# q of a deformable-attention layer by seven products of halves instead of eight, placed in the middle of an even round

## The chip, the cores and the metric

The kernel runs on one core of one Trainium2 chip. The metric is the time of one execution on the device, in microseconds (us). Several runs of the same kernel give a median; one further execution was taken with a profile, and all durations of single instructions come from that one. Engines are named as in the profile: PE is TensorE's matmul, PEld its weight load, DVE is VectorE, ACT is ScalarE, POOL is GpSimd, SP is SyncE, which here only issues DMAs.

## What is computed

Two layers act on x, of 8 images with 512 channels of 64 x 64 pixels, all float32. Cut to what matters here:

```
x = x + attention(group_norm(x))
x = x + bottleneck(group_norm(x))

attention(x):
    q  = w_q @ x                      # 512 x 512 times 512 x 4096 pixels, per image
    t  = gelu(q[every 4th pixel] * w_off1 + b_off1)
    positions = grid + 4 * tanh(w_off2 @ t)        # per group of 64 channels
    f  = bilinear samples of q at the positions    # 256 per group
    k, v = split(w_kv @ f)
    out  = softmax(0.125 * q^T k) v                # 8 heads of 64, 256 keys
    return w_out @ out + b_out
```

The change touches only how q = w_q @ x is formed, and when.

## The kernel before

Everything is float32 and lies in SBUF as 128 partitions x 4 channel blocks x pixels. An image is cut into 8 tiles `t` of 512 pixels (`TP`). An image's tiles lie in nine places of 512 pixels; x of tile t lies in place t + 1 and q of tile t in place t, so q of one tile overwrites x of the tile before it.

**One image's attention is 32 rounds** (8 tiles x 4 pairs of heads, `names`, index `g`, with `r = g % 32`). Round g issues, in this order on PE: the weighted values `pa` (L475), on even rounds the softmax denominators `pn` (L502) of the two rounds before, the logits `ps` of round g + 1 (L457) whose exponentials ACT writes into `es`, and the output projection `pp` (L544) of round g - 6 (`LAG`). DVE adds two exponentials per round (L487), scales, adds the residual (L551) and takes statistics (L554). After each of two places in a round `fill` advances a generator, `next_image`, which carries the work that lies beside: the second layer of the image before (`layer1`), loading and normalising the next image, its q, and its sampling (`sample`).

**q of an image** is `project_q`. Per tile it issues 16 matmuls of 128 x 128 weights on 512 columns (four output blocks of four accumulating matmuls, L252), ACT copies each output block from PSUM (L259), POOL normalises the next tile (L208, four instructions; tile 0 is DVE's), and behind each output block `by_pixel` transposes a quarter of the tile before on PE (four transposes, L226), copies it on ACT or DVE in turn (L236, L234) and stores it to DRAM (L237, on SP's queue) where `sample` gathers from it. At the end of a tile DVE takes the largest magnitude of q (L265). The yields of `project_q` sum to less than the 200 that one call of `fill` may spend, so a whole image's q stands on PE as one unbroken block. For images 2 to 7 this block lies in round 19, between the logits and the output projection. The q of image 0 and of image 1 lie ahead of the first round; that of image 1 is mixed with the sampling of image 0 (L927 to L930).

**Sampling** (`sample`) takes slots that alternate between the two places of a round: gathers issued by POOL (L396), weighing on DVE (L362 to L367), and twice `to_channels`, which transposes on PE (L372) and copies on ACT (L377). In round 30 what is left is drained and `project_k` follows (L410, 16 matmuls of 128 x 128 weights on 256 columns), which reads the copies.

The four buffers `es` (128 x 1024 each) hold exponentials. After the sum of round g's two exponentials on an even round, three of them are free. `wbuf` holds w_q while q is made, and w_kv otherwise. PSUM has two tiles of two banks (`ps_s`), two of one bank (`ps_mm`), and one bank each for `pa` and `pn`.

Of the kernel before, what the change touches and what calls it, by code (L numbers as in the profile page):

```python
# [8 lines left out]
F32 = mybir.dt.float32  # L9
# [7 lines left out]
P = 128  # L17
# [32 lines left out]
def kernel(  # L50
# [50 lines left out]
    def x_tile(b, t):  # L101
        return spot(b, t + 1)

    def q_tile(b, t):
        return spot(b, t)
# [33 lines left out]
        nc.sync.dma_start(wbuf, wv[:, :, part * C : (part + 1) * C])  # L139

    def load_weights_late():
        nc.sync.dma_start(wout, w_outT.rearrange("(cc p) o -> p cc o", p=P))
        nc.sync.dma_start(convw, conv_wT.rearrange("(cc p) o -> p cc o", p=P))
        nc.sync.dma_start(outw, out_wT)
        nc.sync.dma_start(fc2b, fc2_bias)

    def col(k, n=1):
        return vec[:, k : k + n]
# [47 lines left out]
                nc.vector.bn_stats(st[:, cc, t, :], x_tile(b, t)[:, cc, :])  # L196
                yield None

    def project_q(b, st, mq, qd, pools):

        gs = yield from group_stats(st, 0, b)

        qd_px = qd.rearrange("(g h p j) d -> h p g (j d)", g=HEADS, p=P, j=2)

        def normalise(t):
            xt = x_tile(b, t)
            for cc in range(NCC):
                (nc.gpsimd if t else nc.vector).tensor_scalar(  # L208
                    xt[:, cc, :],
                    xt[:, cc, :],  # L210
                    gs[:, 0, cc : cc + 1],
                    gs[:, 1, cc : cc + 1],
                    ALU.subtract,
                    ALU.mult,
                )

        def by_pixel(t, k, bank=(ps_a, "pa")):

            h, ch = divmod(k, 2)
            px = q_tile(b, t)[:, :, 2 * P * h : 2 * P * (h + 1)].rearrange(  # L220
                "p c (n j) -> p c j n", j=2
            )
            pt = bank[0].tile([P, 2, 2 * P], F32, tag=bank[1], name=f"pqt_{b}_{t}_{k}")
            for j in range(2):
                for i in range(2):
                    nc.tensor.transpose(  # L226
                        pt[:, j, i * P : (i + 1) * P], px[:, 2 * ch + i, j, :], ident
                    )
            pool, tag = pools[k % len(pools)]
            qr = pool.tile([P, C], F32, tag=tag, name=f"qr_{b}_{t}_{k}")  # L230
            qr_out = qr.rearrange("p (g j d) -> p j g d", j=2, d=DH)
            qr_in = pt.rearrange("p j (g d) -> p j g d", d=DH)
            if k % 2:
                nc.vector.tensor_copy(qr_out, qr_in)  # L234
            else:
                nc.scalar.copy(qr_out, qr_in)  # L236
            nc.sync.dma_start(  # L237
                qd_px[2 * t + h, :, 4 * ch : 4 * ch + 4, :],
                qr.rearrange("p (g m) -> p g m", g=4),
            )  # L240

        yield None
        normalise(0)
        yield None
        for t in range(NT):
            xt, qt = x_tile(b, t), q_tile(b, t)
            if t + 1 < NT:
                normalise(t + 1)
            for oc in range(NCC):
                pq = ps_mm.tile([P, TP], F32, tag="mm", name=f"pq_{b}_{t}_{oc}")  # L250
                for cc in range(NCC):
                    nc.tensor.matmul(  # L252
                        pq,
                        wbuf[:, cc, oc * P : (oc + 1) * P],
                        xt[:, cc, :],
                        start=(cc == 0),
                        stop=(cc == NCC - 1),
                    )
                nc.scalar.copy(qt[:, oc, :], pq)  # L259
                yield 4  # L260
                if t:
                    by_pixel(t - 1, oc)
                    yield 0.64
            if mq is not None:
                nc.vector.tensor_reduce(  # L265
                    mq[:, t, :], qt, axis=AX.X, op=ALU.max, apply_absolute_value=True
                )
        for q in range(NQ):
            by_pixel(NT - 1, q, ((ps_a, "pa"), (ps_mm, "mm"))[q % 2])
            yield 0.64  # L270
# [8 lines left out]
    def sample(b, qd):  # L279
# [101 lines left out]

        steps = [(h, half, ky) for h in range(2) for half in range(2) for ky in range(2)]

        for slot in range(2 * len(steps) + 4):
            n, odd = divmod(slot, 2)
            if odd and n >= 5 and n % 4 == 1:
                to_channels(n // 4 - 1)
            if odd and 1 <= n <= len(steps):
                weigh(*steps[n - 1], held.pop(0))
            if n < len(steps):  # L390
                h, half, ky = steps[n]
                if not odd:
                    held.append(gp.tile([P, 4, 2, DH], F32, tag="g", name=f"g_{b}_{n}"))
                for i in (2 * odd, 2 * odd + 1):
                    k = h * HEADS + 4 * half + i
                    nc.gpsimd.indirect_dma_start(  # L396
                        held[-1][:, i, :, :].rearrange("p j d -> p (j d)"),
                        None,
                        qd[:, :],
                        bass.IndirectOffsetOnAxis(ap=row[:, ky, k : k + 1], axis=0),  # L400
                    )
            yield None
# [457 lines left out]
    def next_image(b):  # L860

        n = b + 1
        if b:
            free = spot(b - 1, 0)
            first = layer1(b - 1, st1s.pop(b - 1), project_beside, free, free[:, 0:2, :])
            other, blocks = iter(()), ()
            if n < B:
                st = new_stats(0, n)
                blocks = norm_x(n, st)
                other = ready_q(n, st)  # L870


            first_load = 5
            ahead = 4
            slot = 0
            while first:
                if blocks is None and ahead:
                    next(other)
                    ahead -= 1
                if next(first, "end") == "end":  # L880
                    first = None
                if n < B:
                    if first_load <= slot < first_load + NT:
                        load_x(n, (slot - first_load,), nc.gpsimd)
                    if slot == first_load + 2 * NT:
                        load_wq()
                    if phase[0] and (slot == first_load + 3 or slot > first_load + 6):
                        for _ in range(4 if slot == first_load + 3 else 5):
                            if blocks and next(blocks, "end") == "end":
                                blocks = None  # L890
                slot += 1
                yield None
            yield from other
        if n < B:
            yield from sample(n, qds[n])

    qds = {}

    def ready_q(n, st):
        qds[n] = dpool.tile([N * HEADS, DH], F32, tag="qd", name=f"qd_{n}")  # L900
        mqs[n] = small.tile([P, NT, NCC], F32, tag=f"mq{n % 2}", name=f"mq_{n}")
        yield from project_q(n, st, mqs[n], qds[n], both_pools if n > 1 else both_pools[:1])
        if n:
            load_wkv(0)

    with tc.manual_schedule():
        load_x(0)
# [9 lines left out]
        st = new_stats(0, 0)  # L917
        drain(norm_x(0, st))

        for n, step in enumerate(ready_q(0, st)):  # L920
            if n == 3 * NCC:
                st = new_stats(0, 1)
                blocks, other = norm_x(1, st), ready_q(1, st)
            if n >= 3 * NCC and next(blocks, "end") == "end" and 13 * NCC <= n < 13 * NCC + 4:
                next(other)
        room = 0
        for step in sample(0, qds[0]):  # L927
            room += 7
            while room > 0:
                room -= next(other, 7) or 7  # L930
        project_k(0, mqs.pop(0), wkv[0])
        drain(other)
        logits(*names[0])
        project_v(0, wkv[1])
        for g in range(len(names) + LAG):
# [18 lines left out]
                sum_exps(*names[g - 1])  # L954
            if g < len(names):
                add_exps(*names[g])
            if summed:
                invert(*names[g - 1])
            if g + 1 < len(names):
                logits(*names[g + 1])  # L960
# [43 lines left out]
    with tc.If(large > 0):  # L1004
        with tc.For_i(0, B, 1) as i:
            b = "m"
            place[b], region[b] = i, 0
            qd = dpool.tile([N * HEADS, DH], F32, tag="qd", name=f"qd_{b}")
            load_wq()
            load_x(b)  # L1010
            st0, st1 = new_stats(0, b), new_stats(1, b)
            drain(norm_x(b, st0), project_q(b, st0, None, qd, both_pools), sample(b, qd))
            load_wkv(0)
            project_k(b, None)
            project_v(b)
            for t in range(NT):
                attention_max(b, t)
                for oc in range(NCC):
                    load_residual(b, t, oc)
                    project_out(b, t, oc, st1)  # L1020
            drain(layer1_last(b, st1, 1))
# [79 lines left out]
```

## Time and profile before

| what | us |
|---|---|
| median of 3 runs | 3431.71 (3426.51 to 3434.96) |
| the profiled execution, its own time | 3412.4 |
| its span, first to last instruction | 3410.6 |
| PE busy | 3321.9 (97%), 16660 matmuls |
| DVE busy | 1895.9 (56%) |
| ACT busy | 1088.9 (32%) |
| POOL busy | 965.1 (28%) |
| PE busy on the q products, L252 | 920.4, of 2048 records |
| PE busy on the output projection, L544 | 822.9 and 118.6 (two places of the operand) |
| mean granted TensorE clock | 0.99 |

A float32 matmul shows as two records of the same shape, one after the other. "Busy" is the time in which an engine has an instruction running; records of matmuls overlap, so the time that one adds is read from the distance between starts. In the lists, a line gives start, length, engine, source line, operation, output and inputs with partitions x elements, and in brackets how long the engine had been idle before it and what ended that.

### The profile page before, as it was taken

The page shows a single profiled execution, that of the slowest core. Times are in us where ns is not written, and L with a number is a line of the kernel's source. Part 1 is how long each engine was busy: PE and PEld are TensorE (multiplying, and loading weights), DVE is VectorE, ACT ScalarE, POOL GpSimd, SP SyncE. Part 2 cuts the span into 40 slices and gives each one's busy share as a digit, 9 for nine tenths or more (in the row PEclk, how much of TensorE's full clock was granted, in tenths as well). Part 3 has the DMA queues.
Part 4 walks back from the last instruction along what each step waited for, and adds up shares of the span by engine and source line. Part 5 has one row for each costly group of instructions (what it writes and reads, how often), then busy time and mean ns, then how long its engine had stood idle before and what let it go on. Part 6 is the DMA issues. An engine that isn't in the chain of part 4 may idle for free.

```text
span 3410.6 us, 42081 instructions
## 1 busy us (share of the span) xinstructions
PE 3321.9 (97%) x16660; PEld 1242.5 (36%) x16660; DVE 1895.9 (56%) x2958; ACT 1088.9 (32%) x1505; POOL 965.1 (28%) x726
## 2 busy tenths in 40 slices
PE   6999999999999999999999999999999999999996
PEld 3554323335332353324433244322443325433222
DVE  5433765752757427583375923668246682566665
ACT  1223332342333323233233423334233342333420
POOL 6181400162301713027040270302712036210201
PEclk9999999999999999999999999999999999999996
DMA  7222222662326523274333833247232572322713
GB/s 278 74 77 65 81 75 63 197 138 68 118 87 209 110 78 112 75 223 105 93 88 105 217 90 108 88 139 187 70 109 79 183 159 61 107 84 77 125 42 133
DMA packets 293183, 390.35 MB, mean 114 GB/s; under 512 B 17649, under 2 KB 157169, under 8 KB 292977
## 3 DMA queue, kind: packets, MB, share of 16 engines
q1 hardware_dynamic: 240368, 261.72, 23.9%
q0 software_dynamic: 52608, 125.86, 16.6%
q8 instruction: 132, 2.16, 0.3%
q14 instruction: 75, 0.61, 0.1%
HBM read 193.52 MB, written 192.94 MB: 113 GB/s over the span
## 4 chain that ended last, share of the span: by engine, by line
PE 88%; issue 4%; DVE 3%; DMA 2%; ACT 1%; POOL 1%; SPq 0%; ACTq 0%; POOLq 0%; DVEq 0%
PE pq L252 26%; PE pp L544 24%; PE ps L457 12%; PE pa L475 12%; PE pn L502 3%; PE pqt L226 3%; PE py L627 2%; PE pk L410 2%; PE pv L437 2%; PE po L770 2%; DMA out_dram<-spare 1%; DMA out_dram<-image 1%; DMA rn<-rn 1%; DVE wbuf L674 0%; PE po L304 0%
## 5 line engine op out<-in xcount | busy, mean ns | idle before, releaser
L252 PE MATMUL pq<-image,wbuf 128*128 128x512 f32 x2048 | 920.4, 595 | 2.5 <-DVE image L208 1.9
L544 PE MATMUL pp<-image,wout 128*64 128x512 f32 x3584 | 822.9, 601 | 8.9 <-DVE image L530 8.3
L465 ACT ACTIVATE es<-ps 128x1024 f32<-128x1024 f32 x512 | 500.9, 1023 | 264.0 <-PE ps L457 205.1
L252 PEld LDWEIGHTS pq<-image,wbuf 128*128 128x128 f32 x2048 | 374.9, 192 | 391.7 <-issue 379.8
L475 PE MATMUL pa<-es,vt 128*64 128x512 f32 x2048 | 488.2, 597 | 1.7 <-ACT es L465 1.7
L396 POOL DMA_INDIRECT g<-qd,row x256 | 271.5, 1061 | 765.8 <-PE pp L544 443.5
L208 POOL TENSOR_SCALAR image<-image,gs 128x512 f32<-128x512 f32 x224 | 464.8, 2652 | 0.4
L234 DVE COPY qr<-pqt 128x512 f32<-128x512 f32 x128 | 88.4, 691 | 639.5 <-PE pqt L226 634.2
L457 PE MATMUL ps<-image,kt 64*64 64x512 f32 x3584 | 437.9, 602 | 3.9 <-ACT spare L797 3.5
L544 PEld LDWEIGHTS pp<-image,wout 128*64 128x64 f32 x3584 | 237.1, 137 | 551.7 <-issue 462.6
L551 DVE SCALAR_TENSOR_TENSOR image<-pp,vec,image 128x512 f32<-128x512 f32 x224 | 167.3, 747 | 435.8 <-PE pp L544 435.0
L487 DVE TENSOR_TENSOR es<-es,es 128x1024 f32<-128x1024 f32 x256 | 310.6, 1213 | 71.4 <-PE pa L475 71.4
L259 ACT COPY image<-pq 128x512 f32<-128x512 f32 x224 | 131.0, 585 | 684.7 <-PE pq L252 684.7
L482 ACT COPY image<-pa 128x512 f32<-128x512 f32 x224 | 131.4, 586 | 673.5 <-PE pa L475 673.5
L183 POOL TENSOR_TENSOR gs<-ve,nhalf 128x4 f32<-128x4 f32 x16 | 18.0, 1123 | 1014.0 <-DVE ve L182 1014.0
L475 PEld LDWEIGHTS pa<-es,vt 128*64 128x64 f32 x2048 | 137.4, 137 | 297.4 <-issue 276.8
L457 PEld LDWEIGHTS ps<-image,kt 64*64 64x64 f32 x3584 | 114.1, 132 | 315.3 <-issue 178.7
L515 DVE RECIPROCAL rn<-pn 128x512 f32<-128x512 f32 x64 | 214.7, 3355 | 10.1 <-PE pn L502 5.9
L807 POOL DMA_DIRECT2D out_dram<-spare x56 | 68.0, 1214 | 488.1 <-ACT spare L797 469.5
L528 DVE STREAM_SHUFFLE rb<-rn 128x512 f32<-128x512 f32 x256 | 186.8, 730 | 0.1
L226 PEld LDWEIGHTS pqt<-ident,image 128*128 128x128 f32 x896 | 138.0, 203 | 100.9 <-issue 89.2
L196 DVE BATCH_NORM_STATS2 st<-image 128x6 f32<-128x512 f32 x256 | 157.4, 677 | 7.4 <-DMA image<-in_x_dram 7.2
(149 smaller groups left out, 2493.8 us busy)
## 6 DMA issues: line engine op xcount, KB each, us to landing
qd<-qr SPq DMA_DIRECT2D x256, 256.0 KB
image<-in_x_dram SPq DMA_DIRECT2D x112, 512.0 KB
out_dram<-image SPq DMA_DIRECT2D x49, 1024.0 KB
image<-in_x_dram POOLq DMA_DIRECT2D x48, 1024.0 KB, 15.2
out_dram<-spare POOLq DMA_DIRECT2D x56, 512.0 KB, 6.2
out_dram<-part POOLq DMA_DIRECT2D x112, 256.0 KB, 7.8
image<-in_x_dram SPq DMA_DIRECT2D x16, 1024.0 KB
wbuf<-in_w_kvT_dram SPq DMA_DIRECT2D x14, 1024.0 KB
```

Source lines behind the costliest of these rows:

```text
L208: (nc.gpsimd if t else nc.vector).tensor_scalar(xt[:, cc, :], xt[:, cc, :], gs[:, 0, cc : cc + 1], gs[:, 1, cc : cc + 1], ALU.subtract, AL ...
L226: nc.tensor.transpose(pt[:, j, i * P : (i + 1) * P], px[:, 2 * ch + i, j, :], ident)
L252: nc.tensor.matmul(pq, wbuf[:, cc, oc * P : (oc + 1) * P], xt[:, cc, :], start=(cc == 0), stop=(cc == NCC - 1),)
L396: nc.gpsimd.indirect_dma_start(held[-1][:, i, :, :].rearrange("p j d -> p (j d)"), None, qd[:, :], bass.IndirectOffsetOnAxis(ap=row[:, ky, ...
L457: nc.tensor.matmul(ps[k : k + DH, a, :], kt[r : r + DH, hp, kc * P + k : kc * P + k + DH], qt[r : r + DH, hp, :], start=True, stop=True,)
L465: nc.scalar.activation(e, ps, AF.Exp)
L475: nc.tensor.matmul(pa[a * DH : (a + 1) * DH, :], vt[:, kc, hd * DH : (hd + 1) * DH], es[kc][:, a, :], start=(kc == 0), stop=(kc == 1),)
L487: nc.vector.tensor_add(es[0], es[0], es[1])
L515: nc.vector.reciprocal(rn, denominators.pop((b, t)))
L528: nc.vector.stream_shuffle(rb, rn, [2 * (hp % 2) + hp // 2] * 32)
L544: nc.tensor.matmul(pp[r : r + DH, :], wout[:, hp, oc * P + r : oc * P + r + DH], ao[:, hp, :], start=(hp == 0), stop=(hp == NCC - 1),)
L551: nc.vector.scalar_tensor_tensor(xt[:, oc, :], pp, col(V_BOUT + oc), xt[:, oc, :], ALU.add, ALU.add)
```

## The change

q = w @ x is seen as a 2 x 2 product of halves: w in halves of input and output channels (256 each), x in halves of input channels and of pixels. It is formed by seven products in place of eight, with sums formed before and after. A product is four matmuls of 128 x 128 weights on 256 columns, into one PSUM bank.

- Sums of the weights (four of 128 x 512 per image, one in place in `wbuf`) and of x (four per tile, two of them in place) are made on DVE. Sums of products are made on DVE as they leave PSUM: seven additions per tile, each of a bank and an SBUF operand, the first product being copied by ACT.
- The five buffers for sums are three of the four exponentials' buffers. For images 0 and 1 they lie in `wout` and `kt` instead; `wout` is loaded after image 1's q, and image 1 uses image 0's sums of weights.
- Normalising runs two tiles ahead rather than one; tile 1 (POOL) and tile 0 (DVE) are normalised by a generator of their own, ahead of the block.
- The copies behind the transposes are all on ACT, but for two of the last tile.
- The block stands in round 20 of each image (q of images 2 to 7), after the denominators and the sum of exponentials and ahead of the logits of round 21. The reciprocal that belongs to this round (`invert`) is issued inside the block, after tile 2. `sample` follows one round later than before, with one slot less: its second `to_channels` comes directly ahead of `project_k`.

```diff
-    def project_q(b, st, mq, qd, pools):
+    def norm_q(b, st, norms):
         gs = yield from group_stats(st, 0, b)
...
+        norms[b] = normalise
+        yield None
+        normalise(1)
+        normalise(0)
+        yield None
+
+    def project_q(b, normalise, mq, qd, pools, sums, aside=None):
+        qd_px = qd.rearrange("(g h p j) d -> h p g (j d)", g=HEADS, p=P, j=2)
+        s1, s2, s4, t1, t2_ = sums
+        (w11, w21), (w12, w22) = quarters(wbuf)
+        V = nc.vector
+        def of_weights(n):
+            if b == 1:
+                return
+            if n == 1:
+                V.tensor_add(s1, w21, w22)
+            elif n == 2:
+                V.tensor_sub(s2, s1, w11)
+            elif n == 3:
+                V.tensor_sub(w21, w11, w21)
+            else:
+                V.tensor_sub(s4, w12, s2)
+        def of_tile(t, n):
+            (x11, x12), (x21, x22) = quarters(x_tile(b, t))
+            if n == 1:
+                V.tensor_sub(t1, x12, x11)
+            elif n == 2:
+                V.tensor_sub(t2_, x22, t1)
+            elif n == 3:
+                V.tensor_sub(x12, x22, x12)
+            else:
+                V.tensor_sub(x21, x21, t2_)
+        def product(bank, w, xh):
+            for o in range(2):
+                for k in range(2):
+                    nc.tensor.matmul(
+                        bank[:, o * 2 * P : (o + 1) * 2 * P],
+                        w[:, k, o * P : (o + 1) * P],
+                        xh[:, k, :],
+                        start=(k == 0),
+                        stop=(k == 1),
+                    )
+            return bank.rearrange("p (o n) -> p o n", o=2)
...
-            if k % 2:
+            if t == NT - 1 and k % 2:
                 nc.vector.tensor_copy(qr_out, qr_in)
...
+        for n in range(1, 4):
+            of_weights(n)
+            of_tile(0, n)
         for t in range(NT):
+            if t + 2 < NT:
+                normalise(t + 2)
...
+            bank1, bank2 = two_banks(t, 0)
+            nc.scalar.copy(q11, product(bank1, w11, x11))
+            yield 2
+            p6 = product(one_bank(t, 1), s2, t2_)
+            V.tensor_add(q12, q11, p6)
+            pixels(0)
+            yield 2.5
+            p2 = product(bank2, w12, x21)
+            V.tensor_add(q11, q11, p2)
+            of_tile(t, 4)
+            if t == 0:
+                of_weights(4)
+            yield 2
+            p7 = product(one_bank(t, 2), w21, x12)
+            V.tensor_add(q22, q12, p7)
+            pixels(1)
+            yield 2.5
+            bank1, bank2 = two_banks(t, 3)
+            p5 = product(bank1, s1, t1)
+            V.tensor_add(q12, q12, p5)
+            if t + 1 < NT:
+                of_tile(t + 1, 1)
+                of_tile(t + 1, 2)
+            pixels(2)
+            yield 2.5
+            p4 = product(bank2, w22, x21)
+            V.tensor_add(q21, q22, p4)
+            V.tensor_add(q22, q22, p5)
+            if t + 1 < NT:
+                of_tile(t + 1, 3)
+            pixels(3)
+            yield 2.5
+            p3 = product(one_bank(t, 4), s4, x22)
+            V.tensor_add(q12, q12, p3)
...
+            if t == 2 and aside:
+                aside()
...
-        for slot in range(2 * len(steps) + 4):
+        for slot in range(2 * len(steps) + 3):
             n, odd = divmod(slot, 2)
-            if odd and n >= 5 and n % 4 == 1:
-                to_channels(n // 4 - 1)
+            if slot in (11, 18):
+                to_channels(slot // 18)
...
+        drain(norm_q(0, st, norms))
+        st = new_stats(0, 1)
+        blocks, other = norm_x(1, st), norm_q(1, st, norms)
+        for n, step in enumerate(make_q(0, shared)):
+            if n >= 3 * NCC and next(blocks, "end") == "end" and n >= 10 * NCC:
+                next(other, None)
+        drain(other)
+        other = make_q(1, shared)
         room = 0
         for step in sample(0, qds[0]):
-            room += 7
+            room += 6
...
+        drain(other)
+        load_wout()
         project_k(0, mqs.pop(0), wkv[0])
-        drain(other)
...
-            if summed:
+            if r == Q_ROUND and 0 < b < B - 1:
+                tiles = [free_es.pop(0) for _ in range(3)]
+                drain(make_q(b + 1, room_for_sums(tiles), lambda: invert(*names[g - 1])))
+                free_es.extend(tiles)
+            elif summed:
                 invert(*names[g - 1])
```

`quarters(a)[i][j]` is `a[:, 2i:2i+2, 256j:256j+256]`: channel blocks 2i and 2i + 1, columns of half j. `Q_ROUND` is 20. `make_q` makes the tiles of one image's q and calls `project_q`. In the text, p1 to p7 are the seven products, in PE's order p1, p6, p2, p7, p5, p4, p3; p1 is the product of w11 and x11. s1, s2, s4 are sums of weights, t1 and t2 sums of x.

More of the change, by code (lines that the diff above doesn't have):

```diff
@@ L141, in load_weights_late @@
     def load_weights_late():
-        nc.sync.dma_start(wout, w_outT.rearrange("(cc p) o -> p cc o", p=P))
         nc.sync.dma_start(convw, conv_wT.rearrange("(cc p) o -> p cc o", p=P))
@@ L145, in load_weights_late, with load_wout @@
         nc.sync.dma_start(fc2b, fc2_bias)
+    def load_wout():
+        nc.sync.dma_start(wout, w_outT.rearrange("(cc p) o -> p cc o", p=P))
     def col(k, n=1):
@@ L197, in norm_x, with quarters @@
                 yield None
-    def project_q(b, st, mq, qd, pools):
+    def quarters(a):
+        h = C // 2
+        return [[a[:, 2 * i : 2 * i + 2, h * j : h * (j + 1)] for j in range(2)] for i in range(2)]
+    def norm_q(b, st, norms):
         gs = yield from group_stats(st, 0, b)
-        qd_px = qd.rearrange("(g h p j) d -> h p g (j d)", g=HEADS, p=P, j=2)
         def normalise(t):
@@ L215, in normalise, with one_bank, two_banks @@
                 )
+        norms[b] = normalise
[40 more added lines that the diff above has]
+            return bank.rearrange("p (o n) -> p o n", o=2)
+        def one_bank(t, n):
+            return ps_mm.tile([P, TP], F32, tag="mm", name=f"pq_{b}_{t}_{n}")
+        def two_banks(t, n):
+            two = ps_s.tile([P, 2, TP], F32, tag="s", name=f"pq_{b}_{t}_{n}")
+            return two[:, 0, :], two[:, 1, :]
         def by_pixel(t, k, bank=(ps_a, "pa")):
@@ L240, in by_pixel, with pixels @@
             )
-        yield None
-        normalise(0)
-        yield None
+        for n in range(1, 4):
+            of_weights(n)
+            of_tile(0, n)
         for t in range(NT):
-            xt, qt = x_tile(b, t), q_tile(b, t)
-            if t + 1 < NT:
[L248 to L263, printed above, removed]
-            if mq is not None:
-                nc.vector.tensor_reduce(
-                    mq[:, t, :], qt, axis=AX.X, op=ALU.max, apply_absolute_value=True
-                )
+            if t + 2 < NT:
+                normalise(t + 2)
+            (x11, x12), (x21, x22) = quarters(x_tile(b, t))
+            (q11, q12), (q21, q22) = quarters(q_tile(b, t))
+            def pixels(k):
+                if t:
+                    by_pixel(t - 1, k)
+            bank1, bank2 = two_banks(t, 0)
[18 more added lines that the diff above has]
+            V.tensor_add(q12, q12, p5)
+            if t + 1 < NT:
+                of_tile(t + 1, 1)
[11 more added lines that the diff above has]
+            V.tensor_add(q12, q12, p3)
+            if mq is not None:
+                V.tensor_reduce(
+                    mq[:, t, :],
+                    q_tile(b, t),
+                    axis=AX.X,
+                    op=ALU.max,
+                    apply_absolute_value=True,
+                )
+            if t == 2 and aside:
+                aside()
+            yield 2
@@ L869, in next_image @@
                 blocks = norm_x(n, st)
-                other = ready_q(n, st)
+                other = norm_q(n, st, norms)
             first_load = 5
@@ L892, in next_image @@
                 yield None
-            yield from other
+            if n < B:
+                drain(other)
+                while n not in qds:
+                    yield None
         if n < B:
@@ L897, with make_q, room_for_sums @@
     qds = {}
-    def ready_q(n, st):
+    norms = {}
+    Q_ROUND = 20
+    def make_q(n, sums, aside=None):
         qds[n] = dpool.tile([N * HEADS, DH], F32, tag="qd", name=f"qd_{n}")
         mqs[n] = small.tile([P, NT, NCC], F32, tag=f"mq{n % 2}", name=f"mq_{n}")
-        yield from project_q(n, st, mqs[n], qds[n], both_pools if n > 1 else both_pools[:1])
+        pools = both_pools if n > 1 else both_pools[:1]
+        yield from project_q(n, norms[n], mqs[n], qds[n], pools, sums, aside)
         if n:
             load_wkv(0)
+    def room_for_sums(tiles):
+        return [
+            tiles[i // 2][:, i % 2, :].rearrange("p (k o) -> p k o", k=2) for i in range(5)
+        ]
     with tc.manual_schedule():
@@ L918 @@
         drain(norm_x(0, st))
[L920 to L925, printed above, removed]
+        shared = [wout[:, i, :].rearrange("p (k o) -> p k o", k=2) for i in range(3)]
+        shared += [kt[:, 0:2, :], kt[:, 2:4, :]]
+        drain(norm_q(0, st, norms))
[6 more added lines that the diff above has]
+        other = make_q(1, shared)
         room = 0
         for step in sample(0, qds[0]):
-            room += 7
+            room += 6
             while room > 0:
-                room -= next(other, 7) or 7
+                room -= next(other, 6) or 6
+        drain(other)
+        load_wout()
         project_k(0, mqs.pop(0), wkv[0])
-        drain(other)
         logits(*names[0])
@@ L1011 @@
             st0, st1 = new_stats(0, b), new_stats(1, b)
-            drain(norm_x(b, st0), project_q(b, st0, None, qd, both_pools), sample(b, qd))
+            drain(norm_x(b, st0), norm_q(b, st0, norms))
+            drain(project_q(b, norms[b], None, qd, both_pools, room_for_sums(es4)), sample(b, qd))
             load_wkv(0)
```

## Prediction

> **What bounds the kernel now.** First the page's list of busy times, then its costliest groups, then the groups of PE with each shape apart:
>
> ```profile
> PE 3321.9 (97%) x16660; PEld 1242.5 (36%) x16660; DVE 1895.9 (56%) x2958; ACT 1088.9 (32%) x1505; POOL 965.1 (28%) x726
> ...
> L252 PE MATMUL pq<-image,wbuf 128*128 128x512 f32 x2048 | 920.4, 595 | 2.5 <-DVE image L208 1.9
> ...
> L410 PE MATMUL pk<-image,wbuf 128*128 128x256 f32 x224 | 50.2, 382 | 0.0
> ```
>
> PE is the bound, and q is its largest group, with 2.5 us of idle time ahead of 2048 records. So time taken from PE here is time taken from the end, while PE finds no new wait. What a product really costs is read from starts. Timeline of image 2's q block:
>
> ```profile
> 757.33 0.63 PE L226 MATMUL pqt<-ident,spare 128*128 128x128 f32 x4
> 757.80 3.60 PE L252 MATMUL pq<-image,wbuf 128*128 128x512 f32 x8
> ...
> 761.24 0.63 PE L226 MATMUL pqt<-ident,spare 128*128 128x128 f32 x4
> 761.71 3.60 PE L252 MATMUL pq<-image,wbuf 128*128 128x512 f32 x8
> ```
>
> An output block (8 records) with its four transposes repeats every 3.905 us: the same line starts at 749.99, 765.61, 781.22, so a tile is 15.61. The transposes take 0.47 (757.33 to 757.80), the block 3.43, a record 0.429. Nothing waits inside; the block is pure PE.
>
> **The products: 16 matmuls of 512 columns become 28 of 256.** The new shape is in the trace as `pk`, with the same weights' shape. Timeline of ACT where it copies one `pk` per 8 such records:
>
> ```profile
> 538.56 0.38 ACT L417 ACTIVATE kt<-pk 128x256 f32<-128x256 f32 x1 [4.40 <-PE pk L410]
> 540.29 0.38 ACT L417 ACTIVATE kt<-pk 128x256 f32<-128x256 f32 x1 [1.34 <-PE pk L410]
> 542.02 0.38 ACT L417 ACTIVATE kt<-pk 128x256 f32<-128x256 f32 x1 [1.34 <-PE pk L410]
> ```
>
> A step is 1.73, or 0.216 per record: half of 0.429 within 1%. A product (8 records) is thus 1.73, seven 12.1, with four sets of transposes (1.9) 14.0 per tile in place of 15.6. Saved: 15.61 - 13.99 = 1.62 per tile, x 64 tiles = **104 us**. This is the ceiling.
>
> **What DVE gets, per tile.** Rows: an addition with one operand in PSUM repeats after 0.79 (the residual's at 690.18 is followed by the next instruction at 690.97); one of two SBUF operands of 128 x 512 after 0.75 (L528 and L530 at 713.44, 714.20, 714.94, 715.70); the largest magnitude is 2.28 (L265). Seven x 0.79 + four x 0.75 + 2.28 = **10.8 of 14.0 us**. ACT has five copies of 0.585, 2.9, less than before; POOL its four normalisations, 8.24. So PE stays the bound on sums alone, and what counts are deadlines. Count from the end of p3 of a tile, where DVE adds p3 (to 0.9) and reduces (to 3.2). Then p6 ends at 3.5, p2 at 5.7, p7 at 7.4, p5 at 9.6, p4 at 11.8. p4 reads x21 after a sum that DVE can make only when p2 has read it: p2's addition and that sum end at 7.2, p4 starts at 10.1, 2.8 to spare. p7 needs the bank of p3: 4.7 to spare. p6 needs t2, made before the last p4: 3.9. In tile 3 the reciprocal (3.36, L515) comes ahead; the sum for p4 ends at 8.9, 1.2 to spare. DVE may thus be late by 1 to 3 us without PE seeing it. The copies from the one transposes' bank follow 2.2 us apart at least and take 0.6: hidden. The stores of q on SP follow 11% denser, and one stands behind `invert`'s four small DMAs (2.4 us); the copies have four buffers, and a buffer comes free 2.4 us after its copy (163.68 in the trace: ACT waits for the copy that ended at 161.28), so this is hidden too.
>
> **DVE and POOL at once.** The trace shows that sums of two SBUF operands are sometimes held while POOL normalises:
>
> ```profile
> 230.55 1.15 DVE L362 TENSOR_TENSOR g<-g,wt 128x512 f32<-128x512 f32 x1
> ...
> 252.25 0.68 DVE L362 TENSOR_TENSOR g<-g,wt 128x512 f32<-128x512 f32 x1
> 252.97 1.25 DVE L366 TENSOR_TENSOR image<-image,g 128x256 f32<-128x256 f32 x1
> 254.26 0.43 DVE L367 TENSOR_TENSOR image<-image,g 128x256 f32<-128x256 f32 x1
> ```
>
> POOL normalises from 224.22 to 232.46 and from 253.18 on. The first line is 0.47 longer than its like, the third 0.83; four others under POOL (at 199.32, 231.73, 232.19, 254.26) at most 0.05. I take the mean of the six, 0.2 per sum, for four sums: 11.7 us per tile. The far end is each sum held until POOL's four are done: 10.8 + 8.24 = 19.0. The near end is nothing. I stay near the rows.
>
> [...]
>
> **Edges of the block, images 2 to 7.** *Start.* From the end of `pa`, DVE adds exponentials (1.2), then makes s1, t1, s2, t2 (4 x 0.75): ready at 4.45. PE has `pn` (1.0) and p1 (1.75) and waits from 2.8: **+1.65**. Bounds: 0 and 4.45. *End.* Before, the last tile's transposes waited for copies:
>
> ```profile
> 856.33 1.22 PE L226 MATMUL pqt<-ident,image 128*128 128x128 f32 x8 [0.78 <-DVE qr L234]
> ...
> 857.80 1.23 PE L226 MATMUL pqt<-ident,image 128*128 128x128 f32 x8 [0.24 <-ACT qr L236]
> ```
>
> From 854.92 to the next `pp` at 859.12, five sets (2.4) took 4.2. Now p3 stands between the sets, and the first two need neither it nor a busy bank; about 0.4 of wait remains: **-1.4**. *Sampling.* The second `to_channels` stands directly ahead of `project_k`. Before, a `pp` (3.65) hid ACT's copy of 0.59; now PE waits for it with both hand-overs (0.12 from PE to another engine: `pp` gives way at 727.44, its addition starts at 727.56; I take 0.2 each): **+1.0**. The gathers keep the same distance to their weighing, one round. Together per image: 8 x (-1.62) + 1.65 - 1.4 + 1.0 = -11.7, x 6 = **-70**.
>
> POOL's first normalisation now stands ahead of the last stores that `layer1` adds to the output (at 730.08 before); they land some 6 us later, and q21, which overwrites their source, comes 20 us later. Nothing is added. The later load of `wout` has 30 us before its first use.
>
> **Images 0 and 1.** Products save 26. Against it: PE waits for t2 at the very start (normalisation of tile 0 ends at 35.7, four sums 38.7, p1 ends near 36.7): +2. In image 0 DVE also takes image 1's statistics, 7 x 0.61 per tile, over 4.6 tiles: 10.8 + 4.3 = 15.1, 1.1 too much per tile, 5 in all, of which 3 are slack: +2. Between the two images DVE must finish a reduction and two copies that wait for DMAs (2.4 each) before t1 and t2 of image 1, and ACT does the Gelus (5 us) before p1's copy: +4 by that order, bounds 0 and 9. Weighing and gathers among the sums: +2 (bounds 0 and 6; POOL has 8.24 x 0.75 + 5 = 11.2 us for two slots of 10.5). The last copies ahead of `project_k`: +1.5. Together -26 + 11.5 = **-15**.
>
> **Sum.** -70 - 15 = -85: of the profiled 3412.4 that leaves 3327. The median of the runs is 19 us above the profiled execution; taking the same -86 (2.5%) from 3431.7 gives **3345**.
>
> **Rivals.** (1) *DVE is late throughout*: sums held more often, waits between its instructions. At 15.0 per tile PE loses 1.0 of the 1.6, and with the edges some 30 us are gained: 3400. For it: DVE has only 3 us per tile free, and every hand-over between engines passes through it. Against: the six rows. (2) *DVE is the bound and the kernel slower*: each two-operand sum waits for POOL's whole group. It decides from 15.6 per tile, which is 1.2 us of hold per sum; at 19.0 the tiles cost 3.4 more than before, +218: 3650. Against: the longest hold seen is 0.83. (3) *The change does not do what it says*: 256 columns cost more than half of 512 when weights change each time. At 0.245 per record seven products equal eight, and with the edges the time is 3445. Against: `pk` at 0.216.
>
> **How the numbers follow.** Forecast (gain 60 to 105) 0.74; rival 1 (gain 10 to 60) 0.16; rival 2 0.05; rival 3 0.02; edges that eat the gain, 0.03. No wait anywhere gives 3327, less the spread of the runs (5): 3322. Above, half of rival 1 is taken in: 3385. Faster by over 0.3% (10 us, about what a measurement of this kernel can tell): 0.74 + 0.16 = 0.90; within it 0.03 (the edges), slower 0.05 + 0.02 = 0.07.
>
> **What would show it.** PE's q records at 256 columns, 0.216 apart, and tiles at 14.0; if tiles are 14.0, the products and DVE's deadlines are right. PE idle ahead of p4 on DVE's sum in place would be rival 1; DVE lines of two SBUF operands at 1.5 us or more, rival 2; starts 0.24 apart, rival 3. One wait of 1 to 2 us ahead of each image's first p6, and 1 ahead of `project_k`, would show the edges. The forecast is wrong if DVE's busy time inside a tile comes near 14.

## The result, and the profile after

The changed kernel takes **3626.03 us** (median of 4 runs, 3621.36 to 3633.35) where the kernel before took 3429.7 beside it: a ratio of **1.0573** (95% interval 1.0549 to 1.0597). Forecast was 3345, faster. The profiled execution has a span of 3622.0, 211.4 more than before; the medians differ by 196.3, since the execution profiled before (3412.4) was faster than the runs beside it.

The page of the changed kernel: busy times, shares of the chain that ended last, and two of its groups (busy time, mean of one, then the idle time ahead of the group and what ended most of it).

```profile
PE 3297.0 (91%) x18196; PEld 1544.1 (43%) x18196; DVE 2323.4 (64%) x3578; ACT 1051.3 (29%) x1425; POOL 1006.7 (28%) x726
...
PE 76%; DVE 11%; issue 8%; POOL 2%; DMA 2%; ACT 1%; SPq 0%; DVEq 0%; ACTq 0%; POOLq 0%
...
L268 PE MATMUL pq<-image,wbuf 128*128 128x256 f32 x2048 | 491.3, 389 | 10.7 <-DVE spare L341 6.2
...
L293 PE MATMUL pqt<-ident,image 128*128 128x128 f32 x896 | 193.3, 305 | 202.1 <-DVE image L349 67.6
```

PE is busy for less time than before (3297.0 against 3321.9), so the products did save work, and yet the end is later: PE fell from 97% to 91%. Most of the idle time is not ahead of the products but ahead of the **transposes** `pqt`: 202.1 us, against 8.1 in the kernel before:

```profile
L226 PE MATMUL pqt<-ident,image 128*128 128x128 f32 x896 | 141.0, 283 | 8.1 <-DVE qr L234 6.3 <-ACT qr L236 1.7
```

The list of PE's waits in the changed kernel says on whom (us in total, times, longest):

```profile
PE pqt L293 <- DVE image L349: 67.6, 48, 1.8
PE pqt L293 <- DVE image L326: 60.1, 47, 4.8
PE pqt L293 <- DVE image L336: 34.1, 48, 1.2
...
PE pqt L293 <- DVE image L341: 32.3, 48, 0.7
```

L326, L336, L341 and L349 are four of the seven sums as they leave PSUM: with p6 (L326), p7 (L336) and p5 (L341), and the second of the two behind p4 (L349). 48 is 8 images times 6 tiles, the third to the eighth. Timeline of the last tile of image 2, PE first, then DVE (start, length; in brackets the idle time before and what ended it):

```profile
932.85 0.27 PE L293 MATMUL pqt<-ident,image 128*128 128x128 f32 x1
933.86 0.62 PE L293 MATMUL pqt<-ident,image 128*128 128x128 f32 x3 [0.74 <-DVE image L326]
934.32 3.62 PE L268 MATMUL pq<-image,wbuf 128*128 128x256 f32 x16
937.78 0.27 PE L293 MATMUL pqt<-ident,image 128*128 128x128 f32 x1
938.73 0.62 PE L293 MATMUL pqt<-ident,image 128*128 128x128 f32 x3 [0.67 <-DVE image L336]
939.18 1.89 PE L268 MATMUL pq<-es,es 128*128 128x256 f32 x8
...
947.90 0.27 PE L293 MATMUL pqt<-ident,image 128*128 128x128 f32 x1
948.85 1.10 PE L293 MATMUL pqt<-ident,image 128*128 128x128 f32 x7 [0.67 <-DVE image L355]
950.19 1.23 PE L293 MATMUL pqt<-ident,image 128*128 128x128 f32 x8 [0.24 <-ACT qr L303]
```

```profile
933.12 0.69 DVE L326 TENSOR_TENSOR image<-image,pq 128x512 f32<-128x512 f32 x1 [0.52 <-PE pq L268]
936.25 0.69 DVE L330 TENSOR_TENSOR image<-image,pq 128x512 f32<-128x512 f32 x1 [2.45 <-PE pq L268]
...
937.98 0.69 DVE L336 TENSOR_TENSOR image<-image,pq 128x512 f32<-128x512 f32 x1 [0.44 <-PE pq L268]
```

DVE is not late: it is idle for 0.4 to 2.45 us ahead of these sums and starts each 0.2 to 0.3 us after its product. But PE does one transpose of each set of four and then stands until the sum of the product that it has just finished is done (at the last set, both sums). A set takes 0.47 undisturbed (before); here, from its first record to the next product, a set takes 1.47 (932.85 to 934.32), 1.40 and, in the two sets left out, 1.41 and 2.12, which is 4.52 too much: 13.99, as forecast for a tile, and 4.52 are 18.51, and 18.51 is what a tile takes (ACT's copies of p1 start at 894.31, 912.82 and 931.32). The first two tiles take 14.62 and 14.54 (the first has no transposes), the tile with the reciprocal 22.80.

**Theory A.** These are waits without need: the sums write q of tile t, the transposes read q of tile t - 1. The program's order puts each sum just ahead of the set, and what a sum writes is taken as one stretch of addresses per partition, from its first column to its last. A quarter of q is two channel blocks of 256 columns, 4096 columns apart, and between these two stretches lies, in the second block, q of tile t - 1. It fits that the first transpose of a set (lower block) does not wait and the second does, and that tile t = 1 does not wait at its transposes: q of tile 0 lies in `spare`, another tensor. **Rivals**: B, DVE as a whole is late (its work, or POOL's contention); C, the new place of the block costs the time.

### The profile page after: what moved, and what is told of

Its sections match the earlier page's. It is cut to its first block, busy times and chain, and to the rows that moved or that the text cites. A ratio compares the mean times of both kernels' runs of the same rounds, so it can differ in the third digit from the quotient of the medians.

```text
span 3622.0 us, 45896 instructions
## 1 busy us (share of the span) xinstructions
PE 3297.0 (91%) x18196; PEld 1544.1 (43%) x18196; DVE 2323.4 (64%) x3578; ACT 1051.3 (29%) x1425; POOL 1006.7 (28%) x726
## 4 chain that ended last, share of the span: by engine, by line
PE 76%; DVE 11%; issue 8%; POOL 2%; DMA 2%; ACT 1%; SPq 0%; DVEq 0%; ACTq 0%; POOLq 0%
PE pp L643 21%; PE pq L268 19%; PE ps L556 11%; PE pa L574 10%; PE pqt L293 4%; PE pn L601 3%; POOL out_dram L906 2%; PE py L726 2%; PE pk L509 2%; PE pv L536 2%; DMA out_dram<-spare 2%; DVE image L341 1%; DVE image L349 1%; DVE image L348 1%; PE po L869 1%
## 5 line engine op out<-in xcount | busy, mean ns | idle before, releaser
L643 PE MATMUL pp<-image,wout 128*64 128x512 f32 x3584 | 826.1, 599 | 12.4 <-DVE image L629 10.9
L213 POOL TENSOR_SCALAR image<-image,gs 128x512 f32<-128x512 f32 x224 | 505.1, 3353 | 1.1
L268 PE MATMUL pq<-image,wbuf 128*128 128x256 f32 x2048 | 491.3, 389 | 10.7 <-DVE spare L341 6.2
L268 PEld LDWEIGHTS pq<-image,wbuf 128*128 128x128 f32 x2048 | 390.4, 196 | 71.7 <-DVE spare L341 9.5
L293 PE MATMUL pqt<-ident,image 128*128 128x128 f32 x896 | 193.3, 305 | 202.1 <-DVE image L349 67.6
L303 ACT COPY qr<-pqt 128x512 f32<-128x512 f32 x240 | 140.4, 585 | 755.4 <-PE pqt L293 745.6
L268 PE MATMUL pq<-es,es 128*128 128x256 f32 x768 | 182.2, 380 | 8.6 <-DVE es L259 8.6
```

The lines of the kernel that those rows point to most:

```text
L213: (nc.gpsimd if t else nc.vector).tensor_scalar(xt[:, cc, :], xt[:, cc, :], gs[:, 0, cc : cc + 1], gs[:, 1, cc : cc + 1], ALU.subtract, AL ...
L268: nc.tensor.matmul(bank[:, o * 2 * P : (o + 1) * 2 * P], w[:, k, o * P : (o + 1) * P], xh[:, k, :], start=(k == 0), stop=(k == 1),)
L293: nc.tensor.transpose(pt[:, j, i * P : (i + 1) * P], px[:, 2 * ch + i, j, :], ident)
L643: nc.tensor.matmul(pp[r : r + DH, :], wout[:, hp, oc * P + r : oc * P + r + DH], ao[:, hp, :], start=(hp == 0), stop=(hp == NCC - 1),)
```

## The experiments

The kernel before ran again beside each group of kernels; its medians were 3432.32 (beside x1, x2, x3 and x5), 3410.26 (x6 to x9) and 3420.08 (x10), so kernels of different groups are compared by their ratio to it.

### x1_transposes_first

```diff
             p6 = product(one_bank(t, 1), s2, t2_)
-            V.tensor_add(q12, q11, p6)
             pixels(0)
+            V.tensor_add(q12, q11, p6)
```
and so for the other three sets.

> Only the order in the program changes: each set of four transposes is issued ahead of the DVE sums that were issued just before it; nothing is added or left out. Theory A (each set waits for the sum issued just before it, although that sum writes q of tile t and the transposes read q of tile t - 1): the four waits of 0.7 to 1.8 us per tile go, tiles from the third on come from 18.5 to 14.6 to 15.0 us, which are 48 x 3.7 = 178 us, and the tile with the reciprocal loses its 4 us too (6 x 4 = 24): 3415 to 3465 us. Theory B (DVE as a whole is late: too much work, or sums held by POOL): the same sums wait for the same things, so PE's waits move from the transposes to the products, tiles stay near 18: 3590 to 3640. Theory C (the place of the block in round 20 costs the time): no change, 3615 to 3640.

Measured 3440.67, ratio **1.0028** (1.0018 to 1.0038). The four waits are gone, the tile takes 15.01. Timeline of the last tile of image 2:

```profile
850.15 0.63 PE L293 MATMUL pqt<-ident,image 128*128 128x128 f32 x4
851.56 1.99 PE L268 MATMUL pq<-image,wbuf 128*128 128x256 f32 x8 [0.78 <-DVE image L342]
853.39 0.63 PE L293 MATMUL pqt<-ident,image 128*128 128x128 f32 x4
```

Sets of four stand whole again. DVE now starts each sum behind the transposes and not behind the product, the same needless wait turned round. That costs nothing, since DVE had been idle there anyway: 58.4 us ahead of the first sum behind p4 (L349 here), where the changed kernel has 61.0 ahead of the same sum. One wait is left: p4 waits 0.78 for the sum that reads p5, which lies in the other bank of the same two-bank tile. Theories B and C fall as the cause of the loss: DVE's work and the block's place are unchanged here, and 185 us are gone.

### x2_sums_by_block

```diff
-            V.tensor_add(q12, q11, p6)
+            for o in range(2):
+                V.tensor_add(q12[:, o, :], q11[:, o, :], p6[:, o, :])
```
and so for all seven sums; the order is that of the changed kernel.

> The order stays as in the changed kernel; each sum of products is split into two instructions of 128 x 256, one per channel block, so that what one instruction writes is 256 columns in a row instead of two stretches with another tile's q between them. Theory A, in its narrower form (the wait is there because the range of addresses from the first to the last column that a sum writes encloses columns of tile t - 1): the waits ahead of the transposes go or fall to tenths, although the order is the old one; DVE gets 7 more instructions per tile, about 0.1 us each; tiles 14.6 to 15.6: 3430 to 3510 us. If the wait is there only because of the order, whatever the addresses: 3610 to 3650, with the same waits as before on the second of two instructions. Theory B: more instructions on a late DVE, 3640 to 3700. Theory C: 3615 to 3640.

Measured 3414.88, **0.9953** (0.9936 to 0.9969), better than the expectation's 3430 to 3510; tiles of 14.60. Timeline of the last tile of image 2:

```profile
836.57 0.63 PE L298 MATMUL pqt<-ident,image 128*128 128x128 f32 x4
837.04 3.62 PE L273 MATMUL pq<-image,wbuf 128*128 128x256 f32 x16
840.50 0.63 PE L298 MATMUL pqt<-ident,image 128*128 128x128 f32 x4
```

The order is the slow one and the four waits are gone all the same. So it is the enclosed addresses, not the order by itself. The extra instructions (two of 0.42 in place of one of 0.69) cost PE nothing that shows.

### x3_eight_products_in_place

The old loop (16 matmuls of 512 columns per tile, copies on ACT and DVE in turn, no sums) inside the new frame.

> The eight products of 512 columns of the kernel before, with its copies, in all that the change put around them: block in round 20, normalising two tiles ahead, sampling one round later with one slot less, late load of the output weights; no sums. Theory A and theory B: tiles of 15.6 as before, one us of wait at the second turn to channels per image: 3410 to 3440 us. Theory C (the place costs the time): 3590 to 3640.

Measured 3455.11, **1.0072** (1.0056 to 1.0089): 15 us above the range of theory A, far below C's. Tiles are at 15.6, so the 23 us are what the place, with the rest of the frame, costs; the forecast had priced only the wait ahead of `project_k`. By rounds of images 2 to 7 (distances between starts of `pa`, against the trace of before), an image takes 5.2 us more: about 1.7 in round 19, 1.3 in round 22, 1.9 in rounds 24 and 25, 0.75 in round 30. The 1.9 does not come from the place: x1, x2 and x5, of the same group of runs, show 1.6 to 2.1 in these two rounds, x6 to x9, of the group in which the kernel before took 3410.26, show 0.0, and the block stands at the same place in all. Two of the waits that are left, from the timeline:

```profile
1998.51 1.82 PE L523 MATMUL ps<-image,kt 64*64 64x512 f32 x12 [2.10 <-ACT spare L863]
```

```profile
2155.16 1.08 PE L610 MATMUL pp<-image,wout 128*64 128x512 f32 x4 [0.44 <-DVE image L596]
2156.66 1.08 PE L610 MATMUL pp<-image,wout 128*64 128x512 f32 x4 [0.42 <-DVE image L596]
```

The first is round 19: ACT is late there from the second layer's output; in the kernel before, 127 us of q stood in this round, and I take it that they hid this (no run tested it). The second is in round 22: by DVE's order there, the positions of the sampling now stand ahead of an even round's scaling, where they stood in an odd round before.

### x5_order_and_own_banks

x1_transposes_first, and:

```diff
-            two = ps_s.tile([P, 2, TP], F32, tag="s", name=f"pq_{b}_{t}_{n}")
-            return two[:, 0, :], two[:, 1, :]
+            return [
+                ps_s.tile([P, 2, TP], F32, tag="s", name=f"pq_{b}_{t}_{n}_{i}")[:, 0, :]
+                for i in range(2)
+            ]
```

> The order of x1_transposes_first, and p1, p2, p5 and p4 each in a bank that shares its two-bank tile with no other product. Theory A with its second part (a product waits for the reader of the other bank of its tile as well: 0.3 to 0.8 us per tile): tiles at 14.0 to 14.3 us, some 0.6 x 62 = 37 us less than x1_transposes_first: 3375 to 3430 us. If the two banks are told apart: as x1_transposes_first within 10 us. Theory B: 3590 to 3640. Theory C: 3615 to 3640.

Measured 3383.63, **0.9857** (0.984 to 0.9873). The tile takes 13.97. So a product did wait for the reader of its neighbour bank, for 1.04 per tile (15.01 - 13.97), above the 0.3 to 0.8 expected.

### x8_own_banks_alone and x9_two_of_four_first

The banks without the order, and the order for the first two sets only.

> The changed kernel with p1, p2, p5 and p4 each in a bank whose two-bank tile holds no other product; the order stays. Theory A: the four waits ahead of the transposes stay, since they come from SBUF addresses and the order; only the shared bank's 0.2 to 0.7 us per tile go: 3580 to 3620 us. If the shared banks were the cause of most of the loss (x5_order_and_own_banks gained 57 us on x1_transposes_first): 3540 to 3580 us.

> The changed kernel with only the first two of the four sets of transposes per tile issued ahead of the sum before them. Theory A with each wait worth its own share: x1_transposes_first took 185 us off; the two sets moved hold 4.8 longest and 1.2 against 0.7 and 1.8 us, so half to two thirds of the 185 go: 3500 to 3535 us, tiles from the third on about 16.8. If the waits are one lateness of DVE that passes from set to set: next to nothing goes as long as one wait is left, 3590 to 3626 us.

x8 measured 3596.67, **1.0555** (1.0538 to 1.0571): the tile stays at 18.50, only the first two tiles gain (to 13.97 for the second). While PE waits at the transposes anyway, the shared bank costs nothing in these tiles; its wait shows only once the others are gone. x9 measured 3496.44, **1.0251** (1.0235 to 1.0267), tiles at 16.56. Its last two sets:

```profile
853.14 0.27 PE L293 MATMUL pqt<-ident,image 128*128 128x128 f32 x1
854.08 0.62 PE L293 MATMUL pqt<-ident,image 128*128 128x128 f32 x3 [0.67 <-DVE image L341]
...
856.27 0.27 PE L293 MATMUL pqt<-ident,image 128*128 128x128 f32 x1
857.94 0.62 PE L293 MATMUL pqt<-ident,image 128*128 128x128 f32 x3 [1.39 <-DVE image L349]
```

Word for word the waits that these two sets had. Their excess was 0.94 and 1.65, and 13.97 + 2.59 = 16.56: each wait costs its own share, and the four add up. A lateness that passes from set to set would have kept the whole.

### x10_by_block_own_banks

> The changed kernel's order, with the sums of products cut by channel block (as in x2_sums_by_block) and each product in a bank whose two-bank tile holds no other (as in x8_own_banks_alone). Theory A: cut sums and moved sums are two cures of the same wait, and the 0.6 us per tile that x2_sums_by_block still loses is the shared bank; tiles at 13.97 as in x5_order_and_own_banks: 0.98 to 0.99 of the kernel before. If the order itself costs something beside the addresses: tiles at 14.6 or more, 0.995 or more.

Measured 3367.97, **0.9842** (0.9821 to 0.9863), tiles at 13.97: cutting the sums and moving them are two cures of one wait, as A says.

### x6_edges

x5_order_and_own_banks, and:

```diff
+            if t == 0:
+                p2 = product(bank2, w12, x21)
             p6 = product(one_bank(t, 1), s2, t2_)
...
-            of_tile(t, 4)
...
             pixels(1)
+            of_tile(t, 4)
...
-            V.tensor_add(q12, q12, p3)
+            if t < NT - 1:
+                V.tensor_add(q12, q12, p3)
+            else:
+                for o in range(2):
+                    V.tensor_add(q12[:, o, :], q12[:, o, :], p3[:, o, :])
```

> x5_order_and_own_banks with three more steps at its edges, all in the order or cut of instructions: in the first tile p2 ahead of p6; in every tile the sum in place of x21 behind the second set of transposes; in the last tile the sum with p3 cut by channel block. Theory A (waits that come from the order and the enclosed addresses): the wait ahead of the first p6 (1.2 to 1.7 us per image, 13 us in all) falls to at most 0.3, the tile with the reciprocal from 15.25 to 14.0 to 14.5 (5 to 8 us in all), the wait of 0.67 ahead of the last tile's transposes goes (5 us): 3355 to 3370 us. If these waits only move to the next instruction (DVE truly late there): 3375 to 3390 us.

Measured 3334.25, **0.9776** (0.9762 to 0.9789): the fastest version, 2.2% under the kernel before and 0.8% under x5. The expectation, 3355 to 3370, is 0.9775 to 0.982 of the first group's 3432.32; this group's kernel before took 3410.26, so the ratio lies at its lower end. Start and end of an image's block:

```profile
730.33 3.72 PE L268 MATMUL pq<-image,wbuf 128*128 128x256 f32 x16
733.89 1.89 PE L268 MATMUL pq<-es,es 128*128 128x256 f32 x8
...
840.28 1.11 PE L295 MATMUL pqt<-ident,image 128*128 128x128 f32 x8
841.64 1.22 PE L295 MATMUL pqt<-ident,image 128*128 128x128 f32 x8 [0.24 <-ACT qr L305]
```

No wait ahead of p6, 0.24 at the end where there were 0.67 and 0.24, and in images 2 to 7 every tile from the second on at 13.96 or 13.97, that with the reciprocal too (the first, without transposes, 12.1 to 12.4).

### x7_edges_positions_early

x6_edges, with `sample` of images 2 to 7 starting one place earlier and one empty place behind the positions.

> x6_edges, and for images 2 to 7 the Gelus, the offsets' matmuls and the positions one place earlier in their rounds, so that DVE computes the positions in the odd round 21 and not ahead of the scaling in round 22; the gathers keep their places. If the 1.29 us that round 22 lost is DVE's positions ahead of the scaling that the output projection waits for: 6 x 1.3 = 8 us less than x6_edges, less a new wait of some tenths for ACT, whose Gelus now come nearer to the exponentials: 4 to 10 us less. If round 22 waits for something else: the same as x6_edges within 3 us.

Measured 3360.49, **0.9857** (0.9841 to 0.9872): slower than x6 by 0.8% where a gain was expected. The 1.29 of round 22 is gone, so its cause was named rightly. But PE reaches the offsets' matmuls while ACT still makes the Gelus:

```profile
846.74 0.39 PE L412 MATMUL po<-vec,image 128*128 128x4 f32 x2 [0.62 <-ACT image L400]
847.74 2.22 PE L412 MATMUL po<-vec,image 128*128 128x4 f32 x10 [0.62 <-ACT image L400]
849.89 3.68 PE L585 MATMUL pa<-es,vt 128*64 128x512 f32 x8
853.50 2.50 PE L567 MATMUL ps<-image,kt 64*64 64x512 f32 x16
```

This wait comes three times (at 845.73, 846.74 and 847.74), 1.9 in all; the group takes 5.17 up to `pa`, where x6's unbroken one takes 1.87 (1259.96 to 1261.83, image 3), and `pa` behind it takes 3.61 to the next group in place of 1.81. By rounds, an image loses 4.8 there and gains 1.29 in round 22. The wait that was priced at tenths cost more than the one it removed.

## Why the prediction was wrong, point by point

**The step that failed** is "DVE may thus be late by 1 to 3 us without PE seeing it". It counted four deadlines of DVE (p4 on x21, p7 on a bank, p6 on t2, the reciprocal), all of them real uses of data. The four sets of transposes per tile were taken to need nothing from the present tile, and the sharing of two-bank tiles was not looked at. The true slack at a set of transposes was below zero: PE gets there the moment its product ends, and the sum takes 0.7 us more. In all, by the terms that the runs gave, per image (2 to 7):

| term | forecast | measured |
|---|---|---|
| products, 8 tiles | -13.0 | -13.1 (x5, x6: 13.97 in place of 15.61) |
| waits at the transposes, 6 tiles | 0 | +27.2 (6 x 4.54, x8 and x9) |
| tile with the reciprocal | 0 | +4.0 (mean of six, above 18.51) |
| shared bank, first two tiles | 0 | +1.6 (1.04 and 0.57) |
| wait ahead of p6 | +1.65 | +1.7 (first tile's 14.83 less 12.10 and 1.04; 1.4 of it idle) |
| end of the block | -1.4 | -0.3 (four sets in 3.45; before, four of the five in 3.73) |
| wait ahead of `project_k` | +1.0 | +0.7 |
| other rounds | 0 | +3.4 (what is left; 1.3 in round 22, 1.1 in rounds 24 and 25) |
| sum | -11.7 | +25.2 |

The first six rows make 21.1, and the block of an image went from 126.87 to 148.00 (first product to the next work behind it, mean of six). The last two rows are the rest of the mean distance of images 2 to 7, from one `project_k` to the next, which went from 415.33 to 440.55: +25.2. Six images give +151; images 0 and 1 lose +62 up to the second `project_k`, mostly by the same waits (+9 in x1, -10 in x6, where -15 was forecast); the tail gains 1.6: +211, the difference of the spans.

- **Products.** Right: records 0.216 apart, 1.73 a product (806.49 to 808.32, 1.83, stands behind a wait; 744.25 to 745.97 in x6, 1.72, does not), 13.97 a tile.
- **DVE and POOL at once.** The bound was right, the size too large and the spread wrong. The forecast had POOL's four normalisations, 8.24 us, in each tile of 14.0; in images 2 to 7 it normalises in one stretch instead, from ahead of the block's start to about the end of the third tile (first line the kernel before, second the changed kernel, image 2):

```profile
732.17 58.06 POOL L208 TENSOR_SCALAR image<-image,gs 128x512 f32<-128x512 f32 x28
798.04 54.38 POOL L213 TENSOR_SCALAR image<-image,gs 128x512 f32<-128x512 f32 x24
...
L263 DVE TENSOR_TENSOR image<-image,es 128x512 f32<-128x512 f32 x48 | 36.2, 753 | 0.0
```

In these images, 114 sums of two SBUF operands run beside POOL's normalising and average 0.80 (the longest 1.26); the other 102 average 0.69. So some 0.11 are lost in each that meets POOL, and not 0.2 in every one. POOL's normalisations are longer too in this stretch: 2.27 to 2.30 each (mean of an image), where they took 2.07 before, without sums. In the forecast's own lines, the sum of 1.25 at 252.97 starts while POOL still issues a gather (252.19 to 253.13) and ahead of its normalising at 253.18, so that line does not show what held it.
- **Rivals.** Rival 2 had the sign and the wrong mechanism: of the sums of images 2 to 7, none took over 1.26 us, where it needed 1.5 or more. Rival 1 would have shown as idle time ahead of p4 on the sum in place; there is none. No rival named a wait between pieces that share no byte. Rival 3 stays refuted (0.216); by the forecast's own edges its time would be 3451, not 3445.
- **End of the block.** Most of the forecast's -1.4 was missed by a wait of 0.67, which costs the set 0.94: the same kind of wait, on the sum with p3. In x6, without it, the four sets take 2.51 (840.28 to the logits at 842.79), 1.2 less than before.
- **The place.** Round 19's and round 22's waits were not seen; the forecast looked at what moved with the block and not at what the block had covered. The loss in rounds 24 and 25, in part put down to nothing the profile shows ("issue"), goes with the group of runs and not with the kernel; its cause stays open.
- **What the arithmetic was worth.** Without the waits, and with the edges mended, x6 takes 75.4 us off the span against the forecast's 85; x5, with the order and the banks alone, takes 1.4% (49 us).

## What to carry to other kernels

Before counting deadlines by data, list which instruction waits for which, and look for waits between pieces that share no byte: here a piece of a tensor that is written in several stretches stood for all addresses from its first to its last (x2: with the sums cut, tiles of 14.60 in place of 18.51), and a PSUM tile of two banks stood for both (x5: 1.04 us a tile). Cut such a write into pieces that lie in a row, issue the reader first where the writer has time to spare (x1: tiles of 15.01), and give each PSUM bank its own tile. When a long block moves, ask what it had been covering where it was: in x3 an image takes about 1.7 us more in round 19, and that the block had hidden this is a reading that no run tested.

## What the runs showed that was not expected

- A wait that the timeline shows as 0.67 us costs PE 0.94: the set that it breaks takes 1.41 in place of 0.47.
- Needless waits add up to the hundredth (16.56 = 13.97 + 0.94 + 1.65), but one of another kind, the shared bank's 1.04, was wholly hidden behind them.
- In x7 the granted clock is lower behind sparse work on PE. Windows of x7's trace (us, PE busy and records, granted clock, DMA share, GB/s):

```profile
841.00:844.70 3.70, 3.67 (x20) 1.00 0.87 231
844.70:849.90 5.20, 3.32 (x18) 0.80 0.54 188
849.90:853.50 3.60, 3.60 (x9) 0.50 0.00 0
853.50:856.00 2.50, 2.50 (x20) 0.76 0.00 0
```

The clock is 1.00 ahead of the four-column matmuls with their three gaps of 0.62 or 0.63, 0.80 over them and 0.50 in the 3.60 us behind them, where `pa` takes twice its time (3.61 in place of 1.81). In all six images of x7 `pa` is slower behind this group: 2.88 to 3.62. In x6 the output projection behind the unbroken group takes 3.48 or 3.49 (images 3 to 7), as it does ahead of it (1252.78 to 1256.26, image 3). The waits of 0.7 to 1.4 us among the products of the changed kernel did not go with a lower clock: 1.00 from 922 to 946. What sets the clock is not shown by these runs.
